# Mamba in-projection: four taps on 128 rows, two chunks in the array's halves, z, B and C padded to full products

## The chip, the cores and the metric

The kernel runs on one core of a Trainium2 chip. The metric is device time in microseconds (us), the median of several runs. Profiles are of one execution each. PE is the matrix engine, PEld its weight load, DVE the vector engine, ACT the scalar engine, POOL GpSimd, SP the engine that issues nearly all of the DMAs. All data is float32, but for the scores' operands, which are float32r.

## The reference

The input x has 4 images of 128 channels and 64 x 64 points. Layer 0 is a group norm, then layer norms, a depthwise 3 x 3 convolution with GELU and a 1 x 1 product, and a Mamba block on four chunks of 32 channels; layer 1 is attention with 4 heads on 4096 tokens and a mixture of 8 experts, of which each token takes 2. The change concerns the Mamba block's beginning. In the reference's words, cut:

```python
xz = u @ in_proj_w.T                      # 32 channels -> 2 * 64
xin, z = jnp.split(xz, 2, axis=-1)
xin = causal depthwise convolution of xin with conv1d_w (4 taps)
xin = jax.nn.silu(xin + conv1d_b)
x_dbl = xin @ x_proj_w.T                  # -> dt (2), B (16), C (16)
delta = softplus(dt @ dt_proj_w.T + dt_proj_b)
h = exp(delta * A) * h + delta * B * xin  # along the 4096 points, for 64 channels x 16 states
y = sum over states of h * C, + D_skip * xin
out = y * silu(z) @ out_proj_w.T
```

The in-projection and the 4 taps can be one product: a weight for each tap, with the input shifted by 0 to 3 points.

## The kernel before

**Blocks, halves, units, slots.** An image is cut into 8 blocks of 512 points (32 blocks in all). The four chunks are taken two at a time: half p = 0, 1 of the 128 channels; a half's two chunks give 2 x 64 inner channels, which fill 128 partitions. In the kernel before, the inner channels of the two chunks alternate over the partitions (`d = slice(c, P, 2)` in `_laid_out`, line 1466). A unit is a block, a half and two of the 16 states: 512 units. The main loop (lines 1363 to 1416) goes through slots, two for each unit, 1024 in all, and further slots for what is left over. In a slot the main loop writes, in this order: DMAs that have been put off (`flush`), a fetch of rows (`fetch`, line 1374), decays on ACT, `driven` on DVE in even slots (h = B row times du), the attention's score products and their exponentials on ACT, the scan on DVE (even), `read` on DVE (odd: hc = C row times h), the first stage of lane Y, transposes of hc summed into y on PE (`turned_on`), the second stage of lane Y, then the weighted sums of the attention (`weighted`, line 982), and a stage of lane X. Every instruction is chained to the one before it on its engine (`queued`, line 387), so this order is the order on each engine, SP's queue among them.

**Lanes.** Work that isn't scan or attention is written as generators whose `yield`s mark stages. Lane Y makes two stages a slot and lane X two; a task starts when it is at the head of its lane and what it names is done. For each block lane Y has `first_norm` (10 stages), `conv` (26) and `inputs` for the two halves (6 each). Lines 1312 to 1330 put them in order: in(k, 1), which waits for the end of the scan of block k-1's half 1, then the first norm of block k+2 (`upper`), the convolution of block k+1, then in(k+1, 0). At an image's first block `upper` stands last, with 14 stages for the group norm. `until` (line 1285) runs the lanes on at once when a fetch needs a half that isn't done.

**In-projection.** `conv` ends with the normalised block xn on 128 channels and sends four copies into `pairs` (lines 647 to 654): for each half p, 64 rows as they are and 64 rows one point later. `send` puts a DMA on SP at the next `flush`. `inputs` (lines 659 to 708) then makes, for half p, the sum of two products with K = 128 (`inxc`, two taps each) into PSUM bank Y, z with K = 64 (`inz`) into bank X, silu of both on ACT, B and C with 64 columns (`wbc`), and dt with 128 columns (`wdt`). B and C go by ACT into `bc`, by a DMA to `bcd` in DRAM, shape (2 chunks, 8, 2, 1024).

**Rows.** For each unit, `fetched` (line 715) reads the two B rows, and in the next slot the two C rows, back from `bcd` to 128 partitions: each partition gets the 1024 values of its chunk. Four buffers (`rows`) serve, and a fetch is issued three slots ahead of its use. There are 1024 such fetches of 512 KB.

```python
in_=in_of[b, i, p][4][:, n // 2, k, :][None].to_broadcast([DI, 2, 2 * BLK]),
```

**Other transfers with a repeated source.** `finished` reads `inv` (line 1042) as 4 heads, each repeated for 32 partitions; `keys` and `share` repeat too.

```python
out=inv, in_=inverse[b, q][u][:, None, :].to_broadcast([NH, DH, BLK])
```

**Attention.** Score products `sc` are 128*128 (weights' rows and columns). The weighted sums `av` are 128*64: two products side by side, to PSUM partitions 0 to 63 and 64 to 127. 

Of the kernel before, what the change touches and what calls it, by code (L numbers as in the profile page):

```python
# [9 lines left out]
F32 = mybir.dt.float32  # L10
# [7 lines left out]
P = 128  # L18
C = 128
EPS = 1e-5  # L20
BLK = 512
NT = BLK // P
IMG = 64
DI = 64
NST = 16
# [11 lines left out]
def conv_mamba_attn_moe_kernel(ctx: ExitStack, tc: tile.TileContext, t: dict):  # L37
# [37 lines left out]

    late = nc.scalar
    gmat, fc1w = (load(k, eng=late) for k in ("gmat", "fc1w"))
    inx, xdt, dtT, alog = (load(k, pool=scratch, eng=late) for k in ("inx", "xdt", "dtT", "alog"))
    cw = load("cw", [P, 4, P], t["cw"].partition_broadcast(P), pool=scratch, eng=late)
    lnw, lnb, fc1b, lcw, lcb = (load(k, eng=late) for k in ("lnw", "lnb", "fc1b", "lcw", "lcb"))  # L80
    fc2T, fc2b, cb, dtb, dsk = (load(k, eng=late) for k in ("fc2T", "fc2b", "cb", "dtb", "dsk"))
    inz, wbc, wout, projT = (load(k, eng=late) for k in ("inz", "wbc", "wout", "projT"))
# [10 lines left out]
        nc.vector.tensor_scalar_mul(taps[:, k, :], ident, fc1w[:, k : k + 1])  # L93


    inxc = const.tile([P, 2, P], F32, name="inxc")
    for j in range(4):
        r = slice(DI * (j % 2), DI * (j % 2) + DI)
        nc.vector.tensor_mul(inxc[r, j // 2, :], inx[r, :], cw[r, j, :])

    amat = const.tile([P, NST], F32, name="amat")
    nc.scalar.activation(amat, alog, AF.Exp)
# [398 lines left out]


    held = set()
    group_of, y0_of, xn_of, pairs_of, in_of, gated, kqv = {}, {}, {}, {}, {}, {}, {}
    IMAGE = "p (r w) -> p r w"
    group_of[0] = gm0, gr0

# [75 lines left out]
    def conv(b, i):  # L583
        cm = tmp("Y", "cm")
        h = work("Y") if b == 0 else cm
        half = b == i == 0

        def tap(k):
            y0 = y0_rows(b, i, k // 3, k % 3)
            w = fc1w[:, k : k + 1]  # L590

            hr = (cm if half and k > 4 else h).rearrange(IMAGE, w=IMG)
            if b == 0 and not (half and k > 4):
                mm(hr, taps[:, k, :], y0, k == 0, k == (4 if half else 8))
            elif k == 0 or half and k == 5:
                vector.tensor_scalar(hr, y0, w, fc1b, ALU.mult, ALU.add)
            else:
                vector.scalar_tensor_tensor(hr, y0, w, hr, ALU.mult, ALU.add)

        for k in range(0, 5 if half else 9, 2):  # L600
            if b:
                yield
            tap(k)
            if k < (4 if half else 8):
                tap(k + 1)
            if half and k < 4:
                tap(k + 5)
                tap(k + 6)
            if b == 0:
                yield  # L610
                if half and k == 4:
                    vector.tensor_add(cm, h, cm)
                elif k == 8:
                    scalar.activation(cm, h, AF.Identity, bias=fc1b)
            yield
        ps = transposed("Y", by_tile(cm))
        yield
        xt = yield from normalised("Y", by_tile(ps))
        ps = transposed("Y", xt)
        yield  # L620
        g = tmp("Y", "g")
        scalar.activation(g, ps, AF.Gelu, bias=lcb, scale=lcw)
        yield
        ps = work("Y")
        mm(ps, fc2T, g)
        yield
        cm = tmp("Y", "cm")
        vector.scalar_tensor_tensor(
            cm.rearrange(IMAGE, w=IMG), ps.rearrange(IMAGE, w=IMG), fc2b, y0_rows(b, i),
            ALU.add, ALU.add,  # L630
        )
        yield
        ps = transposed("Y", by_tile(cm))
        yield
        xt = yield from normalised("Y", by_tile(ps))
        ps = transposed("Y", xt)
        yield

        xn = mix.tile([P, 3 + BLK], F32, name="xn", bufs=3)
        scalar.activation(xn[:, 3:], ps, AF.Identity, bias=lnb, scale=lnw)  # L640
        if i == 0:
            gpsimd.memset(xn[:, 0:3], 0.0)
        else:
            gpsimd.tensor_copy(xn[:, 0:3], xn_of[b, i - 1][:, BLK : BLK + 3])
        xn_of[b, i] = xn

        pairs = mix.tile([P, 2, 2 + BLK], F32, name="pairs")
        for p in range(2):
            for late in range(2):
                send(  # L650
                    pairs[DI * late : DI * late + DI, p, :],
                    xn[DI * p : DI * p + DI, late : late + 2 + BLK],
                )
        pairs_of[b, i] = pairs
        yield
        yield
        yield

    def inputs(b, i, p):

        xn, pairs = xn_of[b, i], pairs_of[b, i]
        r = slice(DI * p, DI * p + DI)
        while held:
            yield
            yield
        held.add("in")
        ps = work("Y")
        summed(ps, [(inxc[:, j, :], pairs[:, p, 2 * j : 2 * j + BLK]) for j in range(2)])
        pz = work("X")
        mm(pz, inz[r, :], xn[r, 3 : 3 + BLK])  # L670
        yield
        xin = mix.tile([P, BLK], F32, name="xin", bufs=2)
        scalar.activation(xin, ps, AF.Silu, bias=cb)
        zs = mix.tile([P, BLK], F32, name="zs", bufs=4)
        scalar.activation(zs, pz, AF.Silu)
        yield

        pb = work("X")
        mm(pb[0:DI, :], wbc, xin)
        ps = work("Y")  # L680
        mm(ps, wdt, xin)
        yield
        held.clear()
        bc = tmp("Y", "bc")[0:DI, :]
        scalar.copy(bc, pb[0:DI, :])
        bcd = dram.tile([2, NST // 2, 2, 2 * BLK], F32, name="bcd", bufs=4)
        send(bcd.rearrange("c n k (m q) -> (c n k m) q", m=2), bc)

        e = tmp("Y", "e")
        scalar.activation(e, ps, AF.Abs, bias=dtb)  # L690
        scalar.activation(e, e, AF.Exp, scale=-1.0)
        ln = tmp("Y", "ln")
        scalar.activation(ln, e, AF.Ln, bias=1.0)
        delta = mix.tile([P, BLK], F32, name="delta", bufs=2)
        scalar.activation(delta, ps, AF.Relu, bias=dtb)
        yield
        yield

        du = mix.tile([P, BLK], F32, name="du", bufs=2)
        lost = du  # L700
        vector.tensor_scalar(lost, e, 1.0, -1.0, ALU.add, ALU.add)
        vector.tensor_sub(lost, e, lost)
        vector.tensor_add(ln, ln, lost)
        vector.tensor_add(delta, delta, ln)
        vector.tensor_mul(du, delta, xin)
        in_of[b, i, p] = xin, zs, delta, du, bcd
        done.add(("in", b, i, p))
        yield
# [6 lines left out]
    def fetched(unit, k):  # L715

        b, i, p, n = unit
        w = mix.tile([P, 2, BLK], F32, name="rows", bufs=4)
        sync.dma_start(
            out=w.rearrange("p m q -> p (m q)"),  # L720
            in_=in_of[b, i, p][4][:, n // 2, k, :][None].to_broadcast([DI, 2, 2 * BLK]),
        )
        return w

# [585 lines left out]

    X.append((("y0", *blocks[1]), first_norm(*blocks[1], "X"), [("y0", *blocks[0])]))
    for k in range(-2, len(blocks)):
        if 0 <= k:
            b, i = blocks[k]
            Y.append((("in", b, i, 1), inputs(b, i, 1), [("scan", *blocks[k - 1], 1)] if k else []))
        if k + 2 < len(blocks):
            b, i = blocks[k + 2]
            if k + 2 == 0 or i > 0:
                upper(k + 2)
        if 0 <= k + 1 < len(blocks):  # L1320
            b, i = blocks[k + 1]
            below = [("y0", b, i + 1)] if i < NB - 1 else []
            Y.append((("xn", b, i), conv(b, i), before(k + 1, 3) + below))
            Y.append((
                ("in", b, i, 0), inputs(b, i, 0),
                before(k + 1, 2) + ([("scan", *blocks[k], 0)] if k >= 0 else []),
            ))

        if 0 < k + 2 < len(blocks) and blocks[k + 2][1] == 0:
            upper(k + 2)  # L1330
# [113 lines left out]
def _laid_out(i):  # L1444
# [10 lines left out]


    def twice(a):
        return np.repeat(a, 2, axis=0)

    z = np.zeros((P, P), np.float32)  # L1460
    inx, inz = z.copy(), z.copy()
    wout = np.zeros((P, 2, P), np.float32)
    wbc = np.zeros((P, 2, NST // 2, 2, 2), np.float32)
    xdt, dtT = np.zeros((4, P), np.float32), np.zeros((4, P), np.float32)
    for c in range(2):
        d = slice(c, P, 2)
        for p in range(2):
            s = slice(64 * p + 32 * c, 64 * p + 32 * c + 32)
            inx[s, d] = c0["in_proj_w"][:DI].T
            inz[s, d] = c0["in_proj_w"][DI:].T  # L1470
            wout[d, p, s] = c0["out_proj_w"].T

        wbc[d, c] = c0["x_proj_w"][2:].reshape(2, NST // 2, 2, DI).transpose(3, 1, 0, 2)
        xdt[2 * c : 2 * c + 2, d] = c0["x_proj_w"][:2]
        dtT[2 * c : 2 * c + 2, d] = c0["dt_proj_w"].T
# [5 lines left out]
    for h in range(NH):  # L1481
# [12 lines left out]
        "lcw": col(c0["lc_ln_w"]), "lcb": col(c0["lc_ln_b"]),  # L1494
        "fc1w": c0["lc_fc1_w"].reshape(C, 9), "fc1b": col(c0["lc_fc1_b"]),
        "fc2T": c0["lc_fc2_w"].T, "fc2b": col(c0["lc_fc2_b"]),
        "inx": inx, "inz": inz,
        "cw": twice(c0["conv1d_w"]).T,
        "cb": col(twice(c0["conv1d_b"])),
        "xdt": xdt, "dtT": dtT, "dtb": col(twice(c0["dt_proj_b"])),  # L1500
        "wbc": wbc.reshape(P, -1), "alog": twice(c0["A_log"]),
# [28 lines left out]
```

## Time and profile before

| what | value |
|---|---|
| median of 3 runs | 5217.45 us (5217.27 to 5228.61) |
| profiled execution | 5213.97 us, its span 5211.8 us |
| PE, DVE, ACT busy | 91%, 74%, 72% |
| mean granted clock of PE | 0.957 |
| DMA: bytes, mean rate | 1131.60 MB, 217 GB/s |
| rows<-bcd | 1024 transfers of 512.0 KB |
| ps_Y<-pairs,inxc | 256 matmul records, busy 131.4 us |
| ps_X<-xn,w_inz | 128 records, 64*128, 74.6 us |
| ps_X<-xin,w_wbc | 128 records, 128*64, 73.0 us |

An f32 product of 512 columns shows as two matmul records. In the lists of instructions "out<-in" are the program's tile names, and "[idle before <-releaser]" is the idle time ahead of an instruction and what ended it. `SPq` rows are DMAs that SP issues.

### The profile page before, as it was taken

The page shows a single profiled execution, that of the slowest core. Times are in us where ns is not written, and L with a number is a line of the kernel's source. Part 1 is how long each engine was busy: PE and PEld are TensorE (multiplying, and loading weights), DVE is VectorE, ACT ScalarE, POOL GpSimd, SP SyncE. Part 2 cuts the span into 40 slices and gives each one's busy share as a digit, 9 for nine tenths or more (in the row PEclk, how much of TensorE's full clock was granted, in tenths as well). Part 3 has the DMA queues.
Part 4 walks back from the last instruction along what each step waited for, and adds up shares of the span by engine and source line. Part 5 has one row for each costly group of instructions (what it writes and reads, how often), then busy time and mean ns, then how long its engine had stood idle before and what let it go on. Part 6 is the DMA issues. An engine that isn't in the chain of part 4 may idle for free.

```text
span 5211.8 us, 62608 instructions
## 1 busy us (share of the span) xinstructions
PE 4743.5 (91%) x20684; PEld 2298.3 (44%) x20684; DVE 3834.8 (74%) x5780; ACT 3749.6 (72%) x5700; POOL 423.0 (8%) x483
## 2 busy tenths in 40 slices
PE   4567899999999999899999999999999999999997
PEld 2333444444444444444444444444444444443443
DVE  6888767777788878888788887887788877751332
ACT  4456777788787787678888787778777787756543
POOL 1111111100000000001000000000000001000000
PEclk7678999999999999899999999999999999999998
DMA  4556567676766667767766667767766666754542
GB/s 126 180 186 207 210 208 244 227 236 242 234 225 228 230 223 239 244 231 246 258 228 226 233 224 231 259 229 253 264 233 228 219 229 219 265 179 156 185 130 72
DMA packets 451692, 1131.60 MB, mean 217 GB/s; under 512 B 51985, under 2 KB 135330, under 8 KB 451362
## 3 DMA queue, kind: packets, MB, share of 16 engines
q1 hardware_dynamic: 447296, 1125.96, 64.4%
q8 instruction: 166, 2.72, 0.2%
q10 hardware_dynamic: 4066, 1.57, 0.2%
q14 instruction: 164, 1.34, 0.1%
HBM read 967.12 MB, written 143.39 MB: 213 GB/s over the span
## 4 chain that ended last, share of the span: by engine, by line
PE 56%; DVE 17%; ACT 13%; DMA 6%; issue 5%; POOL 2%; SPq 1%; DVEq 0%; ACTq 0%; POOLq 0%
PE av L406 23%; PE sc L406 13%; PE ps_X L406 9%; DVE h L406 6%; PE ps_Y L406 5%; PE y L406 5%; ACT pT L406 4%; ACT L406 3%; DMA ks<-kd 2%; DVE hc L406 2%; ACT xt L406 1%; ACT e L406 1%; DMA rows<-bcd 1%; POOL rsX L406 1%; DVE stX L406 1%
## 5 line engine op out<-in xcount | busy, mean ns | idle before, releaser
L406 ACT ACTIVATE pT<-sc 128x1024 f32<-128x1024 f32 x2048 | 1985.0, 1023 | 941.0 <-PE sc L406 939.6
L406 PE MATMUL av<-pT,v 128*64 128x512 f32 x8192 | 2002.9, 610 | 11.4 <-DVE avs L406 11.4
L406 PE MATMUL sc<-qs,ks 128*128 128x512 f32 x4096 | 1294.3, 436 | 67.5 <-DMA ks<-kd 35.8
L406 DVE TENSOR_TENSOR_SCAN h<-da,state,h 128x1025 f32<-128x1025 f32 x512 | 1204.1, 2352 | 96.1 <-ACT h L406 62.5
L406 PEld LDWEIGHTS sc<-qs,ks 128*128 128x128 f32 x4096 | 701.9, 190 | 795.9 <-ACT pT L406 258.1
L406 PEld LDWEIGHTS av<-pT,v 128*64 128x64 f32 x8192 | 500.2, 137 | 846.4 <-issue 816.9
L406 ACT ACTIVATE da<-delta,amat 128x512 f32<-128x512 f32 x1024 | 743.1, 730 | 1.9
L406 PE MATMUL y<-ident,hc 128*128 128x128 f32 x4096 | 628.8, 285 | 64.5 <-DVE hc L406 64.5
L406 DVE TENSOR_TENSOR hc<-rows,h 128x1024 f32<-128x1024 f32 x512 | 624.2, 1219 | 15.8 <-PE y L406 5.9
L406 DVE TENSOR_TENSOR h<-rows,du 128x1024 f32<-128x1024 f32 x512 | 623.4, 1218 | 14.2 <-DMA rows<-bcd 14.1
L406 PEld LDWEIGHTS y<-ident,hc 128*128 128x128 f32 x4096 | 522.8, 147 | 236.9 <-issue 84.6
L406 ACT ACT_TABLE_LOAD x319 | 409.3, 1283 | 19.5 <-DVE zs L406 14.3
L406 POOL TENSOR_TENSOR rsX<-rsX,mhalf 128x4 f32<-128x4 f32 x92 | 203.7, 2214 | 2533.5 <-DVE rsX L406 2448.8
L406 POOL TENSOR_TENSOR rsY<-rsY,mhalf 128x4 f32<-128x4 f32 x100 | 130.6, 1306 | 2070.4 <-DVE shiftY L406 1558.8
L406 DVE TENSOR_TENSOR avs<-av,prev 128x512 f32<-128x512 f32 x96 | 66.1, 689 | 254.2 <-PE av L406 242.8
L406 PE MATMUL ps_X<-share,w_ew 128*128 128x512 f32 x432 | 217.0, 625 | 9.0 <-DVE share L406 8.8
L406 ACT ACTIVATE xt<-ps_Y,shiftY,rsY 128x128 f32<-128x128 f32 x380 | 143.9, 469 | 84.9 <-POOL shiftY L406 77.2
L406 DVE TENSOR_TENSOR share<-share,xf 128x1024 f32<-128x1024 f32 x128 | 155.9, 1218 | 20.5 <-DMA share<-sharesX 14.8
L406 ACT COPY state<-h 128x2 f32<-128x2 f32 x448 | 88.8, 198 | 92.8 <-DVE h L406 92.8
L406 DVE SCALAR_TENSOR_TENSOR cm<-y,w_fc1w,cm 128x512 f32<-128x512 f32 x195 | 144.9, 743 | 8.0 <-ACT y L406 4.5
L406 PE MATMUL ps_Y<-pairs,inxc 128*128 128x512 f32 x256 | 131.4, 638 | 15.0 <-DMA pairs<-xn 9.4
L406 PEld LDWEIGHTS ps_X<-share,w_ew 128*128 128x128 f32 x432 | 74.0, 191 | 149.4 <-issue 97.4
(248 smaller groups left out, 3435.9 us busy)
## 6 DMA issues: line engine op xcount, KB each, us to landing
rows<-bcd SPq DMA_DIRECT2D x1024, 512.0 KB
ks<-kd SPq DMA_DIRECT2D x192, 512.0 KB
qs<-qd SPq DMA_DIRECT2D x161, 512.0 KB
share<-sharesX SPq DMA_DIRECT2D x108, 512.0 KB
v<-vd SPq DMA_DIRECT2D x192, 256.0 KB
ks<-kd SPq DMA_DIRECT2D x128, 256.0 KB
avd<-avs SPq DMA_DIRECT2D x96, 256.0 KB
prev<-avd SPq DMA_DIRECT2D x96, 256.0 KB
```

The lines of the kernel that those rows point to most:

```text
L406: return lambda *args, **kw: queued(op(*args, **kw))
```

## The change

- `inxc` holds one weight [128, 64] in place of two [128, 128]: its rows are 32 channels x 4 taps. `windows` copies, for half p, each chunk's 32 channels with four shifts into 128 rows of `fours`; `conv` sends those of half 0, and `inputs` of half 0 sends those of half 1. The number of sends stays four a block, each of 256 KB.
- `inputs` makes one product of 64 columns for each chunk, to the two halves of PSUM's partitions. A `yield` ahead of it moves it from the first stage of a slot to the second, that is directly ahead of `weighted`. z comes a stage later. A call has 8 stages for 6.
- z's weight has all 128 rows, one matrix for each half, with zeros for the other half. B and C have 128 columns, of which 64 are zeros; only 64 rows of the result are used.
- The inner channels of the two chunks lie one after the other over the partitions (`d = slice(DI * c, DI * c + DI)`). So the source of the rows fetch is written as (2 chunks, 64 repeats, 1024).
- In lane Y, `upper(k + 2)` stands ahead of in(k, 1).

```diff
-    inxc = const.tile([P, 2, P], F32, name="inxc")
-    for j in range(4):
-        r = slice(DI * (j % 2), DI * (j % 2) + DI)
-        nc.vector.tensor_mul(inxc[r, j // 2, :], inx[r, :], cw[r, j, :])
+    inxc = const.tile([P, DI], F32, name="inxc")
+    nc.vector.tensor_mul(inxc, inx, cw)
...
-        pairs = mix.tile([P, 2, 2 + BLK], F32, name="pairs")
-        for p in range(2):
-            for late in range(2):
-                send(
-                    pairs[DI * late : DI * late + DI, p, :],
-                    xn[DI * p : DI * p + DI, late : late + 2 + BLK],
-                )
-        pairs_of[b, i] = pairs
-        yield
-        yield
-        yield
+        windows(b, i, 0)
+        yield
+        yield
+        yield
+
+    def windows(b, i, p):
+        fours = mix.tile([P, 2, BLK], F32, name="fours")
+        for c in range(2):
+            r = slice(DI * p + DI // 2 * c, DI * p + DI // 2 * (c + 1))
+            src = xn_of[b, i][r, :]
+            src = bass.AP(src.tensor, src.offset, (src.ap[0], (1, 4), (1, BLK)))
+            send(fours[:, c, :], src)
+        fours_of[b, i, p] = fours
...
         held.add("in")
+        yield
         ps = work("Y")
-        summed(ps, [(inxc[:, j, :], pairs[:, p, 2 * j : 2 * j + BLK]) for j in range(2)])
-        pz = work("X")
-        mm(pz, inz[r, :], xn[r, 3 : 3 + BLK])
+        for c in range(2):
+            mm(ps[DI * c : DI * c + DI, :], inxc, fours[:, c, :])
         yield
         xin = mix.tile([P, BLK], F32, name="xin", bufs=2)
         scalar.activation(xin, ps, AF.Silu, bias=cb)
+        pz = work("X")
+        mm(pz, inz[:, p, :], xn[:, 3:])
+        yield
         zs = mix.tile([P, BLK], F32, name="zs", bufs=4)
         scalar.activation(zs, pz, AF.Silu)
+        if p == 0:
+            windows(b, i, 1)
         yield
 
         pb = work("X")
-        mm(pb[0:DI, :], wbc, xin)
+        mm(pb, wbc, xin)
...
-            in_=in_of[b, i, p][4][:, n // 2, k, :][None].to_broadcast([DI, 2, 2 * BLK]),
+            in_=in_of[b, i, p][4][:, n // 2, k, :][:, None].to_broadcast([2, DI, 2 * BLK]),
...
-        if 0 <= k:
-            b, i = blocks[k]
-            Y.append((("in", b, i, 1), inputs(b, i, 1), [("scan", *blocks[k - 1], 1)] if k else []))
         if k + 2 < len(blocks):
             b, i = blocks[k + 2]
             if k + 2 == 0 or i > 0:
                 upper(k + 2)
+        if 0 <= k:
+            b, i = blocks[k]
+            Y.append((("in", b, i, 1), inputs(b, i, 1), [("scan", *blocks[k - 1], 1)] if k else []))
...
-        d = slice(c, P, 2)
+        d = slice(DI * c, DI * c + DI)
```

More of the change, by code (lines that the diff above doesn't have):

```diff
@@ L77, in conv_mamba_attn_moe_kernel @@
     gmat, fc1w = (load(k, eng=late) for k in ("gmat", "fc1w"))
-    inx, xdt, dtT, alog = (load(k, pool=scratch, eng=late) for k in ("inx", "xdt", "dtT", "alog"))
-    cw = load("cw", [P, 4, P], t["cw"].partition_broadcast(P), pool=scratch, eng=late)
+    inx, cw, xdt, dtT, alog = (
+        load(k, pool=scratch, eng=late) for k in ("inx", "cw", "xdt", "dtT", "alog")
+    )
     lnw, lnb, fc1b, lcw, lcb = (load(k, eng=late) for k in ("lnw", "lnb", "fc1b", "lcw", "lcb"))
@@ L503, in conv_mamba_attn_moe_kernel @@
     held = set()
-    group_of, y0_of, xn_of, pairs_of, in_of, gated, kqv = {}, {}, {}, {}, {}, {}, {}
+    group_of, y0_of, xn_of, fours_of, in_of, gated, kqv = {}, {}, {}, {}, {}, {}, {}
     IMAGE = "p (r w) -> p r w"
@@ L657, in conv @@
         yield
+    def windows(b, i, p):
[6 more added lines that the diff above has]
+        fours_of[b, i, p] = fours
     def inputs(b, i, p):
-        xn, pairs = xn_of[b, i], pairs_of[b, i]
-        r = slice(DI * p, DI * p + DI)
+        xn, fours = xn_of[b, i], fours_of.pop((b, i, p))
         while held:
@@ L1457, in twice @@
     def twice(a):
-        return np.repeat(a, 2, axis=0)
-    z = np.zeros((P, P), np.float32)
-    inx, inz = z.copy(), z.copy()
+        return np.concatenate([a, a])
+    inz = np.zeros((P, 2, P), np.float32)
     wout = np.zeros((P, 2, P), np.float32)
-    wbc = np.zeros((P, 2, NST // 2, 2, 2), np.float32)
+    wbc = np.zeros((P, 4, NST // 2, 2, 2), np.float32)
     xdt, dtT = np.zeros((4, P), np.float32), np.zeros((4, P), np.float32)
     for c in range(2):
-        d = slice(c, P, 2)
+        d = slice(DI * c, DI * c + DI)
         for p in range(2):
             s = slice(64 * p + 32 * c, 64 * p + 32 * c + 32)
-            inx[s, d] = c0["in_proj_w"][:DI].T
-            inz[s, d] = c0["in_proj_w"][DI:].T
+            inz[s, p, d] = c0["in_proj_w"][DI:].T
             wout[d, p, s] = c0["out_proj_w"].T
@@ L1496, in _laid_out @@
         "fc2T": c0["lc_fc2_w"].T, "fc2b": col(c0["lc_fc2_b"]),
-        "inx": inx, "inz": inz,
-        "cw": twice(c0["conv1d_w"]).T,
+        "inx": np.repeat(c0["in_proj_w"][:DI].T, 4, axis=0), "inz": inz,
+        "cw": np.tile(c0["conv1d_w"].T, (DI // 2, 1)),
         "cb": col(twice(c0["conv1d_b"])),
```

## The prediction

> **What bounds the kernel now.** I read the page's busy times first, then its DMA parts. PE is busy 91% of the span, DVE 74%, ACT 72%; the 16 DMA engines average 64% in the one queue SP feeds.
>
> ```profile
> PE 4743.5 (91%) x20684; PEld 2298.3 (44%) x20684; DVE 3834.8 (74%) x5780; ACT 3749.6 (72%) x5700; POOL 423.0 (8%) x483
> ...
> q1 hardware_dynamic: 447296, 1125.96, 64.4%
> ...
> rows<-bcd SPq DMA_DIRECT2D x1024, 512.0 KB
> ```
>
> The reader is to see two things: PE is nearest to its limit, and half of all bytes (1024 x 512 KB = 537 of 1126 MB) are the rows fetches. Next comes the answer by stages: prologue, scan (slots 0 to 1023, the ones that fetch rows), and the attention left over.
>
> ```profile
> 0.00:73.00 73.00, 31.50 (x110) 16.20 (x110) 27.17 (x112) 16.76 (x30) 11.18 (x40) 0.86 0.28 68
> 73.00:4600.00 4527.00, 4144.49 (x18328) 2040.77 (x18330) 3637.71 (x5203) 3430.39 (x5335) 399.21 (x430) 0.96 0.69 230
> 4600.00:5212.00 612.00, 567.47 (x2248) 241.34 (x2244) 169.92 (x466) 302.44 (x336) 12.60 (x13) 0.96 0.41 136
> ```
>
> Columns: stretch, us, then busy us of PE, PEld, DVE, ACT, POOL, granted clock, DMA share, GB/s. A slot of the scan lasts 4527/1024 = 4.42 us, and PE has 4.05 us of work in it. DMA is 69% busy and spread over 16 engines, so rows is rarely late: the waits of DVE show it last only 7 times, 14.1 us in all. Third, the timeline of PE around one in-projection:
>
> ```profile
> 2422.49 1.19 PE L406 MATMUL sc<-qs,ks 128*128 128x512 f32 x4
> 2423.53 1.88 PE L406 MATMUL ps_Y<-pairs,inxc 128*128 128x512 f32 x4
> 2425.33 1.12 PE L406 MATMUL ps_X<-xn,w_inz 64*128 64x512 f32 x2
> 2426.39 1.94 PE L406 MATMUL av<-pT,v 128*64 128x512 f32 x8
> 2428.25 1.20 PE L406 MATMUL sc<-qs,ks 128*128 128x512 f32 x4
> 2429.38 1.07 PE L406 MATMUL ps_X<-xin,w_wbc 128*64 128x512 f32 x2
> 2430.38 1.13 PE L406 MATMUL ps_Y<-xin,wdt 128*128 128x512 f32 x2
> 2431.35 1.47 PE L406 MATMUL y<-ident,hc 128*128 128x128 f32 x12
> ```
>
> Two records are one f32 product. Start to start, PE never idles here; these slots are PE's. Last, the answer on the tile inv, because its source has the shape that the changed rows fetch gets (below):
>
> ```profile
> L406 SPq DMA_DIRECT2D inv<-inverse x32: 517/557/832, 1311.2 to 5156.6; - x32
> ...
>   DMA inv<-inverse: 61.7, 20
> ```
>
> DVE stood still 61.7 us for these 32 transfers of 256 KB, more than four times what 1024 rows transfers cost it.
>
> **What the Trainium skill says.** "DMA: Bandwidth & Descriptors", section "Why a DMA increments its semaphore by 16 and not by 1": a transfer is split over k engines, k being the largest number up to 16 that divides the sizes of the slowest dimension (other than 1) of both access patterns, and only those k engines post a completion. The trace agrees. Counting the completion events after each issue, the trace has 16 for every rows, ks, aT and share transfer, 9 for sharesX<-prT (8 rows), and 5 for inv<-inverse, total<-avs and den<-total, whose slowest dimension is 4: k engines and one write by the issuer. The same page, section "Rules for kernel authors", warns that an outermost dimension of c < 16 confines the whole DMA to at most c engines. "TensorEngine Tiling (Array Packing)", section "Key Properties": tiles run in parallel, and changing the tiling mode drains the array. The trace agrees: two av products side by side take 1.86/2 = 0.93 us (2426.39 to 2428.25 for two such pairs), hardly more than one full product (1.80/2 = 0.90 us), and w_inz (64*128) takes 1.06.
>
> **The change, part by part.**
>
> *Taps in the array's halves.* Two full products (1.80 us) become one pair in halves, placed by the added yield directly ahead of av, which has the same 128*64 mode: 0.93 us and no further switch. Saves 0.87 us for each of 64 calls.
>
> *z, B, C padded.* w_inz 1.06 to 0.90, saves 0.16. w_wbc stood between full products: sc before it ran 1.13 instead of some 1.04, it took 1.00 and wdt 0.97; full, 1.80 for both: saves 0.26. Together 1.29 us x 64 = 83 us of PE. PE is idle 468 us of the span, so not each of these slots is PE's; at about two thirds it is worth 55 us, if PE stays the bound. From both sides: 0 to 83.
>
> *Windows.* Per block SP issues four transfers as before (two per half), of 256 KB instead of 128.5 KB: 512 packets of 2048 B (median 84 ns) for 256. 256 more x 32 blocks x 84 ns / 16 = 43 us more per DMA engine. Their sources have 32 partitions, so 16 engines. The second half's pair is issued from inside the first call, which ends two slots later; the call for it then waits for the scan anyway. Free at today's 69%. PE waited 9.4 us for pairs in all; the mm now comes half a slot later, so no more than that.
>
> *Two more stages a call, order of the lane.* Lane Y makes two stages a slot, 64 a block, and needs 52 instead of 48. upper(k+2) fills the wait for the scan that head-of-lane in(k,1) had. At the three batch borders in(.,1) ends about the slot where it is fetched; at most a few us each. I take 0; below zero at most some 10 us.
>
> *Set-up.* One multiplication for four, 0.9 us less on DVE; inx and cw 256 KB smaller, inz and wbc 96 KB larger. 0.
>
> *Rows.* The halves of the partitions now hold the two chunks one after the other, so the source of rows<-bcd goes from (64 repeats, 2 chunks, 1024) to (2 chunks, 64 repeats, 1024). This is inv's form, (4 heads, 32 repeats, 512), with 2 in place of 4. So k goes from 16 to 2: each of two engines moves 64 packets of 4096 B instead of 8. A 4096 B packet takes 159 ns (median; 10th percentile 156; mean 195, with 16 engines competing). The packets in flight at once never stay much above 16, so an engine serves one at a time. One fetch: 64 x 159 ns = 10.2 us, against a slot of 4.42 us that needs one fetch. It can't be hidden by more buffers: it is throughput. Four rows buffers keep two or three fetches queued on these two engines, so they hardly starve.
>
> **The sum for the two engines in the scan.** Rows: 1024 x 10.18 = 10,420 us. All else that they carry: 0.69 x 4527 = 3,124 us of packets per engine now, less rows' own 131,072 x 195 ns / 16 = 1,594, is 1,530; at the uncontended 159/195 of that, 1,250. The k = 4 transfers already lie on the low engines (24 packets more than an even share for each of 64 total and some 27 inv): 24 x 91 x 84 ns = 183. The windows: 43. Sum 11,896 us. With prologue 73 and the tail 612, whose slots fetch no rows: 12,581. Idle of the two engines: SP waits in order for a transfer's landing before it can issue the next (bcd before rows 64 times, sharesX, total, inverse 32 times each or less, 160 chains); such a landing now queues behind rows ("DMA: Bandwidth & Descriptors", "Queues, rings and completion order": each engine takes its descriptors in ring order; no view of before shows a queue that long). Nothing at best, one fetch each at worst, 160 x 10.2 = 1,630. I take a quarter, 400, since the scan's calls are mostly done several slots ahead of their fetch. 12,980; less what PE saves in the tail, 0. The profiled execution has 5211.8 us of span and 2.2 around it, 5213.97 in all, 3.5 (0.07%) under the median of 5217.45, far below the uncertainty here. Forecast: **12,980 us**.
>
> Low end: packets at 156 ns (10,224) and no idle: 12,385, say 12,300. High end: all chains drain, 12,581 + 1,630 = 14,210, and some gap between packets: 14,400.
>
> **The rivals.**
>
> *Faster: rows keeps its 16 engines.* If destination and source are split jointly in a way that inv doesn't show, the change is what its words say, and PE's 83 us are worth two thirds: 5,214 - 55 = 5,159 us. The mechanism's place is the split of the 1024 fetches; it decides from k = 8: 32 KB x 2 a fetch, 16 x 159 ns = 2.5 us, plus 1.4 us of other traffic, 3.9 us, fits the 4.42 us slot; at k = 4 5.1 + 1.4 us don't. Against it: inv, total and den, all three. Chance 0.04.
>
> *Starved engines.* k = 2, but the chains drain at each landing and the FIFO order delays ks and v behind three fetches (30 us, where they are asked for three slots ahead), so PE and with it hc are late too: 14,400 to 16,500, say 15,200 us. For it: one queue, in order. Against it: rows waits only for DVE, and DVE's and PE's work of a slot is 4 us of nearly 12. Chance 0.09.
>
> *More than two engines at a time or faster packets:* a split over 4 (5.1 us of rows) gives 73 + 1024 x 5.09 + 1,476 + 612 = 7,370 us. For it only that a form not seen may be split otherwise. Chance 0.03. Within 0.3% is left with 0.01.
>
> The forecast's own case has 0.83; within it the range above. Chances: faster by over 0.3% 0.04, within 0.3% 0.01, slower 0.95 (0.3% is about what a measurement of this kernel can tell from no change).
>
> **What would show it.** Right: 3 completion events for each rows transfer; DMA rows<-bcd as the wait of DVE's h and hc by thousands of us (1024 x some 7 us); PE busy below 40%; the DMA rows at 1 to 2 tenths through the scan, about 88 GB/s on average, and the tail as long as now; ps_Y<-fours pairs starting about 0.93 us before av, w_inz and w_wbc at 0.90. A slot of the scan near 12 us. Wrong: 16 events, or PE still near 91% (first rival); idle stretches of DMA in the scan of more than 10% of it (second). The lane's steps are wrong if PE waits for fours more than 10 us in all before any rows are late.

## The result, and the profile after

| | median us | ratio to before, 95% |
|---|---|---|
| before | 5217.36 (5214.05 to 5228.61, 6 runs) | 1 |
| changed | 12880.01 (12874.39 to 12886.01, 6 runs) | 2.4686 (2.4661 to 2.4711) |
| forecast | 12,980, range 12,300 to 14,400 | |

The change made the kernel 2.47 times as slow. The same parts of the page that were read before, for the changed kernel: busy times, the DMA line of the 40 slices, the queue's share, and the chain that ended last.

```profile
PE 5585.2 (43%) x20684; PEld 2729.1 (21%) x20684; DVE 3890.8 (30%) x5777; ACT 3777.0 (29%) x5700; POOL 396.6 (3%) x483
...
DMA  1111222222222222222222222222222222223243
...
q1 hardware_dynamic: 441152, 1142.62, 25.9%
...
DMA 64%; SPq 20%; PE 9%; DVE 5%; ACT 1%; issue 1%; POOL 0%; DVEq 0%; ACTq 0%; POOLq 0%
```

DVE and ACT have the work that they had (3891 for 3835 us, 3777 for 3750), and PE has the same 20684 records, which take 5585 us for 4744 at a lower clock. No engine got more to do; they wait. The trap is the DMA line: 2 tenths look like an idle resource. A mean over 16 engines of 2 tenths is also what two full engines and fourteen nearly empty ones give, and the chain says DMA for 64% and SP's queue (SPq) for 20%. By stages, with the columns as in the prediction:

```profile
0.00:73.00 73.00, 30.87 (x110) 15.94 (x110) 26.59 (x110) 18.29 (x32) 11.18 (x40) 0.86 0.29 73
73.00:12200.00 12127.00, 4960.92 (x18254) 2459.52 (x18256) 3680.89 (x5193) 3445.25 (x5318) 372.82 (x430) 0.68 0.25 87
12200.00:12881.00 681.00, 593.44 (x2322) 253.66 (x2318) 183.27 (x474) 313.42 (x351) 12.61 (x13) 0.92 0.39 133
```

The whole loss is in the scan; prologue and tail are as they were (the last rows fetch is issued at 12,241.5, so 42 us of the last line still belong to the scan). PE's mean granted clock fell to 0.68 in the scan; how its clock goes with its pauses is taken up at the end of the experiments. The answer on the tile rows, the fetches and then DVE's waits for them, first before, then after:

```profile
L406 SPq DMA_DIRECT2D rows<-bcd x1024: 512/519/1810, 73.1 to 4591.4; - x171
...
  DMA rows<-bcd: 14.1, 7
```

```profile
L405 SPq DMA_DIRECT2D rows<-bcd x1024: 487/3427/17143, 71.6 to 12241.5; - x171
...
  DMA rows<-bcd: 4690.6, 674
```

DVE waits for rows 674 times, 4691 us in all, where it waited 7 times, 14.1 us. The lines of the fetches (min, median and max in ns) hold what I had not looked for: to issue one such transfer takes SP 3.4 us in the median instead of 0.52.

Three counts from the trace's lists of DMA packets and completion events. The packets in flight are those of the queue that SP feeds, over the scan, which I take from 73 us to 12,253 us, 11.5 us after the last fetch is issued:

```
completion events a rows transfer   before 16    after 3 (two engines and the issuer)
packet of 4096 B, median            159 ns       160 ns
packets in flight, after            2: 9241 us   0 or 1: 61 us   3 and more: 2878 us
```

For three quarters of the scan exactly two packets are in flight: two engines work, fourteen have nothing to do.

### The profile page after: what moved, and what is told of

Same layout as the page of the kernel before. It is cut to its first block, busy times and chain, and to the rows that moved or that the text cites. A ratio compares the mean times of both kernels' runs of the same rounds, so it can differ in the third digit from the quotient of the medians.

```text
span 12880.9 us, 62527 instructions
## 1 busy us (share of the span) xinstructions
PE 5585.2 (43%) x20684; PEld 2729.1 (21%) x20684; DVE 3890.8 (30%) x5777; ACT 3777.0 (29%) x5700; POOL 396.6 (3%) x483
## 4 chain that ended last, share of the span: by engine, by line
DMA 64%; SPq 20%; PE 9%; DVE 5%; ACT 1%; issue 1%; POOL 0%; DVEq 0%; ACTq 0%; POOLq 0%
DMA rows<-bcd 37%; SPq L405 20%; DMA ks<-kd 10%; PE av L405 4%; DMA sharesX<-prT 3%; PE sc L405 3%; DMA fours<-xn 2%; DMA inv<-inverse 2%; DMA share<-sharesX 2%; DMA gn<-in_x 2%; DVE h L405 2%; DMA xr<-in_xtok 2%; PE ps_X L405 1%; DMA prev<-avd 1%; PE ps_Y L405 1%
## 5 line engine op out<-in xcount | busy, mean ns | idle before, releaser
L405 PE MATMUL sc<-qs,ks 128*128 128x512 f32 x4096 | 1518.4, 500 | 3785.4 <-DMA ks<-kd 3773.9
L405 PE MATMUL av<-pT,v 128*64 128x512 f32 x8192 | 2316.9, 689 | 16.5 <-DVE avs L405 15.7
L405 PEld LDWEIGHTS sc<-qs,ks 128*128 128x128 f32 x4096 | 847.6, 228 | 4620.3 <-issue 4062.3
L405 PE MATMUL y<-ident,hc 128*128 128x128 f32 x4096 | 781.0, 331 | 943.7 <-DVE hc L405 839.2
L405 PEld LDWEIGHTS y<-ident,hc 128*128 128x128 f32 x4096 | 635.9, 174 | 1222.9 <-DVE hc L405 892.4
L405 PEld LDWEIGHTS av<-pT,v 128*64 128x64 f32 x8192 | 597.3, 157 | 1059.0 <-issue 1026.2
L405 PE MATMUL ps_X<-share,w_ew 128*128 128x512 f32 x432 | 267.9, 752 | 371.7 <-DVE share L405 371.7
L405 PE MATMUL ps_Y<-fours,inxc 128*64 128x512 f32 x256 | 136.0, 978 | 394.2 <-DMA fours<-xn 394.2
L405 ACT COPY h<-state 128x1 f32<-128x1 f32 x512 | 97.8, 191 | 615.6 <-DVE hc L405 615.5
L405 PE MATMUL ps_X<-w_wp,aT 128*128 128x128 f32 x216 | 51.6, 414 | 410.4 <-DVE aT L405 410.4
```

Of the source, the lines that this page charges most:

```text
L405: return lambda *args, **kw: queued(op(*args, **kw))
```

## Experiments: is it the rows fetch's split?

The theory: the split of the rows fetch over two engines is the whole loss, as throughput. Rivals: other edits of the change have a part in it; the order of the one queue and its latencies set the time.

**One line put back.** The source's repeats outside again, in the changed kernel.

```diff
-            in_=in_of[b, i, p][4][:, n // 2, k, :][:, None].to_broadcast([2, DI, 2 * BLK]),
+            in_=in_of[b, i, p][4][:, n // 2, k, :][None].to_broadcast([DI, 2, 2 * BLK]),
```

> The changed kernel with one line put back: the rows fetch's source is again (64 repeats, 2 chunks, 1024). The two chunks then reach the partitions in turn, while the changed layout has them one after the other, so this kernel multiplies partly by the other chunk's B and C; number and size of all instructions are those of the changed kernel. Theory (the loss is the split of the rows fetch over two engines, all else of the change saves PE time): 16 completion events a transfer, 5159 us, between 5110 and 5215. Rival (windows, stages or lane order lose something too): over 5220 us. Rival (the line has nothing to do with it): near 12880 us.

Measured: 5215.12 us, ratio 0.9994 (0.9985 to 1.0003), 16 events a transfer. The line is the loss. That the time is at the very end of the theory's range (5215), with no gain at all, is the subject of the next section.

**The line and its layout alone,** in the kernel before.

```diff
-            in_=in_of[b, i, p][4][:, n // 2, k, :][None].to_broadcast([DI, 2, 2 * BLK]),
+            in_=in_of[b, i, p][4][:, n // 2, k, :][:, None].to_broadcast([2, DI, 2 * BLK]),
...
-        return np.repeat(a, 2, axis=0)
+        return np.concatenate([a, a])
...
-        d = slice(c, P, 2)
+        d = slice(DI * c, DI * c + DI)
```

> The kernel before with only the chunks laid one after the other over the partitions and the rows fetch as (2 chunks, 64 repeats, 1024). Theory (two engines carry all rows): as slow as the whole change, 12800 to 13000 us, with two packets in flight for some 9200 us of the scan. Rival (the other edits take a good part of the loss): below 11000 us. Rival (the line is harmless): near 5217 us.

Measured: 12,922.49 us (one run), two packets in flight for 9378 us up to the last fetch's issue. Taps, padding, windows and stages have no part in the loss.

**Four and eight engines.** Each row of bcd is written two or four times, so that the source's outermost dimension is 4 or 8 (here for two copies):

```diff
-        bcd = dram.tile([2, NST // 2, 2, 2 * BLK], F32, name="bcd", bufs=4)
-        send(bcd.rearrange("c n k (m q) -> (c n k m) q", m=2), bc)
+        bcd = dram.tile([NST, 2, 2, 2, BLK], F32, name="bcd", bufs=4)
+        for c in range(2):
+            for m in range(2):
+                send(
+                    bcd[:, c, :, m, :],
+                    bc[32 * c + m : 32 * c + 32 : 2, None, :].to_broadcast([NST, 2, BLK]),
+                )
...
+            in_=in_of[b, i, p][4][n + k].rearrange("c r m q -> (c r) (m q)")[:, None]
+            .to_broadcast([4, 32, 2 * BLK]),
...
```

> The changed kernel, with each B and C row written twice to DRAM, so that the source of a rows fetch is (2 chunks x 2 copies, 32 repeats, 1024): slowest dimension 4. Theory (throughput of k engines, 64/k x 2 packets of 159 ns an engine and fetch): 5 completion events, 1024 x 5.1 us of rows and some 1750 us of other packets on the low engines, with prologue and tail 7650 us, between 7350 and 7900. Rival (latency or the order of the queue, not the engines' throughput, sets the time): well over 8500 us, since all waits in order stay. Rival (split doesn't matter): 12880 us.

> The changed kernel with each B and C row written four times: slowest dimension 8. Theory (throughput of k engines): 9 completion events; rows 1024 x 2.55 us and some 1900 us of other packets on the low eight engines are 4500 us, just what the scan of the 16-engine kernels takes, so 5350 to 5700 us. Rival (order and latency set the time, as their waits are the same for each k): over 6000 us.

Measured, one run each: 7925.87 us with 5 events, and 6125.23 us with 9. The events are as expected; both times lie past my ranges, four engines by 26 us and eight by 425 us, where the rival's "over 6000 us" is what came. So the times alone don't decide; what the traces have in flight does. Up to the last fetch, exactly k packets are in flight for 9241 us (k = 2), 4257 us (k = 4) and 2007 us (k = 8): each doubling takes away more than half, as throughput must. Fewer than k are in flight for only 61, 104 and 380 us of the scan, so the k engines stay full and latency sets little of the time. And more than k are in flight, with other traffic beside the rows, for 2878, 2864 and 3042 us; this hardly changes, and with eight engines it is over half of the scan. My sums took 1750 and 1900 us for all other packets and 159 ns for a packet of 4096 B, which took 191 and 227 ns in the mean. With eight engines the fetch isn't hidden; DVE's h still waited 235.8 us for it.

**Sixteen engines by copies, and two fetches.** Eight copies in the way shown (outermost 16), or no copies and a fetch for each chunk:

```diff
-        sync.dma_start(
-            out=w.rearrange("p m q -> p (m q)"),
-            in_=in_of[b, i, p][4][:, n // 2, k, :][:, None].to_broadcast([2, DI, 2 * BLK]),
-        )
+        for c in range(2):
+            sync.dma_start(
+                out=w[DI * c : DI * c + DI].rearrange("p m q -> p (m q)"),
+                in_=in_of[b, i, p][4][c, n // 2, k, :][None].to_broadcast([DI, 2 * BLK]),
+            )
```

> The changed kernel, with each B and C row written eight times to DRAM, so that the source of a rows fetch is (2 chunks x 8 copies, 8 repeats, 1024). Theory (engine count): 16 completion events and the PE part of the change comes through, 5170 us, between 5110 and 5230; the copies add 57 MB of writes, some 150 us of the 16 engines' time in a scan that has room. Rival (reading one row many times in a run is slow by itself): over 5500 us.

> The changed kernel with each rows fetch issued as two transfers of 64 partitions, one for each chunk, each from a single row repeated 64 times. Theory (engine count): both have 16 completion events; as fast as with the repeats outside, 5215 us, plus what 1024 more issues of some 0.52 us on SP's queue cost: between 5205 and 5260. Rival (two half-height transfers on the same engines are slower in themselves, as the eightfold copies were): over 5300 us.

Measured: 5342.41 us, ratio 1.0254 (1.0236 to 1.0271), and 5340.64 us, ratio 1.0238 (1.0222 to 1.0254). Both have 16 events and are rid of the loss, but for some 125 us, which put both over my ranges (up to 5230 and 5260). In both, a packet of 4096 B took longer, 241 and 243 ns on average for 194 with the repeats outside. I took that for the price of engines that read one row over and over, and tried it in the changed kernel:

```diff
-            in_=in_of[b, i, p][4][:, n // 2, k, :][:, None].to_broadcast([2, DI, 2 * BLK]),
+            in_=in_of[b, i, p][4][0, n // 2, k, :][None].to_broadcast([P, 2 * BLK]),
```

> The changed kernel with every rows fetch reading one row (the first chunk's) 128 times, in one transfer over 16 engines; the second chunk's channels get the first's B and C. Theory (packets slow down when engines read one row over and over: 241 ns for 4096 B in the copies, 243 in the two fetches, 194 with the two rows in turn): 5340 us, packets of 240 ns. Rival (the half-height transfers and the copies each have their own cost): 5215 us, packets of 195 ns.

Measured: 5216.79 us, ratio 0.9999 (0.9991 to 1.0008), packets 195 ns. That theory fell. What the copies and the half-height transfers pay 125 us for stays open; that both share one cause isn't shown either.

## Experiments: where did PE's gain go?

With the line put back, PE's shorter products are there, and the time is that of before. The timeline of PE in that kernel:

```profile
2414.49 1.08 PE L405 MATMUL ps_Y<-fours,inxc 128*64 128x512 f32 x4
2415.40 1.89 PE L405 MATMUL av<-pT,v 128*64 128x512 f32 x8
2417.22 1.20 PE L405 MATMUL sc<-qs,ks 128*128 128x512 f32 x4
2418.25 1.02 PE L405 MATMUL ps_X<-xn,w_inz 128*128 128x512 f32 x2
2419.11 1.47 PE L405 MATMUL y<-ident,hc 128*128 128x128 f32 x12
...
2424.58 1.02 PE L405 MATMUL ps_X<-xin,w_wbc 128*128 128x512 f32 x2
2425.44 1.02 PE L405 MATMUL ps_Y<-xin,wdt 128*128 128x512 f32 x2
2426.30 0.60 PE L405 MATMUL y<-ident,hc 128*128 128x128 f32 x4
```

From start to start the pair in halves, z, B and C, and dt take 0.91, 0.86, 0.86 and 0.86 us, 3.49 for the 4.83 of before (1.80, 1.06, 1.00, 0.97). By this one call the estimate is 1.34 x 64 = 86 us. But PE's busy time fell by 55 us only, at a mean clock of 0.950 for 0.957 (by estimate 0.007 x 5216 = 37 us), and its idle time grew from 468 to 528 us. Four kernels take the edits apart.

**Lane order as before,** in the kernel with the line put back:

```diff
+        if 0 <= k:
+            b, i = blocks[k]
+            Y.append((("in", b, i, 1), inputs(b, i, 1), [("scan", *blocks[k - 1], 1)] if k else []))
         if k + 2 < len(blocks):
             b, i = blocks[k + 2]
             if k + 2 == 0 or i > 0:
                 upper(k + 2)
-        if 0 <= k:
-            b, i = blocks[k]
-            Y.append((("in", b, i, 1), inputs(b, i, 1), [("scan", *blocks[k - 1], 1)] if k else []))
```

> The changed kernel with the repeats outside (5215 us), and lane Y's order as in the kernel before: in(k, 1) ahead of the next first norm. Theory (PE's 95 us went into later waits because slots are also bound by ACT and DVE, whatever the order of the lane): 5205 to 5225. Rival (the new order moved norms to slots where PE waits for them, 122 us for xt instead of 69): 5150 to 5190.

**Six stages as before,** in the same kernel:

```diff
         held.add("in")
-        yield
         ps = work("Y")
...
+        pz = work("X")
+        mm(pz, inz[:, p, :], xn[:, 3:])
         yield
         xin = mix.tile([P, BLK], F32, name="xin", bufs=2)
         scalar.activation(xin, ps, AF.Silu, bias=cb)
-        pz = work("X")
-        mm(pz, inz[:, p, :], xn[:, 3:])
-        yield
```

> The changed kernel with the repeats outside (5215 us), and the six stages of the kernel before: taps and z at once in the first stage of a slot, not next to the weighted sums. The pair in halves then stands between full products, some 0.1 us a call more on PE. Theory (PE's gain is lost in any case): 5205 to 5230. Rival (the two added stages cost what PE gained): 5150 to 5190.

**Both edits.**

> The changed kernel with the repeats outside (5215 us), and both the six stages and the lane order of the kernel before: of the change there remain the windows, the taps in halves, the padding and the layout, and every stage falls where it fell before. Theory (the moved stages, by either edit, eat PE's 95 us, since slots have other limits): 5125 to 5175 us, below the 5185 us of the padding alone. Rival (windows and halves gain nothing wherever they stand): 5185 us or more.

**The padding alone,** in the kernel before:

```diff
-        mm(pz, inz[r, :], xn[r, 3 : 3 + BLK])
+        mm(pz, inz[:, p, :], xn[:, 3:])
...
-        mm(pb[0:DI, :], wbc, xin)
+        mm(pb, wbc, xin)
...
```

The rest of this edit makes the two weights larger and fills them with zeros.

> The kernel before with only z's weight on 128 rows and B and C's on 128 columns, padded with zeros; order, layout and fetches as before. PE has 0.16 + 0.26 us less for each of 64 calls, 27 us. Theory (little of PE's gain reaches the end of a slot): 5205 to 5218. Rival (the padding's gain is real and the moved stages eat it in the whole change): 5185 to 5200.

| kernel | us | ratio, 95% | POOL busy us | rsY power, median ns | PE idle us | PE busy at half clock, us |
|---|---|---|---|---|---|---|
| before | 5217 | 1 | 423.0 | 1007 | 468 | 300 |
| padding alone | 5184.80 | 0.9936 (0.9922 to 0.9950) | 423.4 | 1008 | 473 | 284 |
| line put back, stages and order of before | 5185.15 | 0.9935 (0.9922 to 0.9949) | 423.0 | 1007 | 487 | 271 |
| line put back | 5215.12 | 0.9994 (0.9985 to 1.0003) | 455.3 | 1981 | 528 | 353 |
| line put back, order of before | 5217.65 | 0.9997 (0.9988 to 1.0005) | 494.7 | 1918 | 517 | 385 |
| line put back, six stages | 5228.05 | 1.0015 (1.0009 to 1.0022) | 515.3 | 1919 | 517 | 338 |

Two things follow. The padding brings 33 us, all of what PE saves by it (its busy time falls by 34 us): where nothing is moved, PE's time counts nearly one for one, and my theory for that run (little reaches the end of a slot) was wrong. And windows with taps in halves bring nothing beyond it where they stand between full products, as the rival of that run had it; there the pair takes 1.00 and 1.53 us in two calls and not 0.91. With the added stages, or with the new order, or with both, the kernel loses the padding's gain as well, 30 to 43 us. That these two edits take the gain is shown; by what way is less clear.

The table shows a first candidate, POOL. Lane Y's norms raise the variance to the power -0.5 there. The answer on the tile rsY, first before, then with the line put back (min/median/max ns):

```profile
L406 POOL TENSOR_TENSOR rsY<-rsY,mhalf x100: 1006/1007/1992, 22.7 to 5168.4; 128x4 f32<-128x4 f32 x100
```

```profile
L405 POOL TENSOR_TENSOR rsY<-rsY,mhalf x100: 1007/1981/1992, 21.0 to 5168.5; 128x4 f32<-128x4 f32 x100
```

The Trainium skill, "SBUF — State Buffer", section "Who interferes with whom", says that a DVE instruction with two SBUF inputs contends with a GpSimd instruction that reads SBUF. The traces agree: a power took 1.9 to 2.0 us where a DVE product of two SBUF tiles (hc, h, share) was running when it began, 1.0 us beside none of these (43 of 44 powers before), and 1.0 to 1.5 us where the power began first. Before, 27 of the 100 powers met such a product running, with the line put back 65: the moved stages put the norms there. PE's wait for xt, the norm's next step, went from 68.8 to 122.0 us. To price it, the padding alone got a second, unused power ahead of the real one in lane Y:

```diff
+        if lane == "Y":
+            junk = small.tile([P, NT], F32, name="junk")
+            gpsimd.tensor_tensor(junk, rs, mhalf, ALU.pow)
         gpsimd.tensor_tensor(rs, rs, mhalf, ALU.pow)
...
```

> The padding alone (5185 us), with a second power of -0.5 on POOL, its result unused, ahead of the real one in lane Y's norms, 95 times: each adds 1.0 us to the way from DVE to ACT's xt, or 2.0 us where it falls beside a DVE product of two SBUF tiles. Theory (where the moved stages put 72 instead of 39 of the 100 powers beside such a product, these 33 x 1 us cost the 30 to 40 us that are missing; time on POOL in the norms counts nearly one for one): 5250 to 5340 us. Rival (the longer powers are a by-product, the norms have slack): below 5200 us.

Measured: 5254.40 us, ratio 1.0070 (1.0054 to 1.0086), 70 us over the padding alone for 133 us more on POOL. The waits of PE, first of the padding alone, then with the second power:

```profile
PE ps_Y L406 <- ACT xt L406: 69.6, 21, 7.7
PE y L406 <- DVE hc L406: 64.6, 21, 9.2
```

```profile
PE ps_Y L406 <- ACT xt L406: 139.6, 50, 10.1
PE y L406 <- DVE hc L406: 65.0, 21, 9.2
```

PE's wait for xt grew by 70 us. In the two profiled executions, which are 74 us apart, PE's idle time grew by 62 us (473 to 535) and its busy time by 12. So in this kernel a us on POOL costs about half a us; my theory's "nearly one for one" was too much, though the time is just inside its range. By that price the 32, 72 and 92 us more of POOL in the last three rows of the table would be 17, 38 and 48 us, against 30, 33 and 43 us lost.

The waits do not bear this out for the last two. The second power showed up as PE's wait for xt. This wait is 122.0 us with the line put back, where it is 70.2 with stages and order of before, but only 80.3 with the order of before and 97.7 with six stages. (For the first of the three it would do: 52 us more, where PE's idle time grew by 41.) What grew most in the other two is another wait each. First with stages and order of before, then with the order of before alone, then with six stages alone:

```profile
PE sc L405 <- ACT pT L405: 46.4, 140, 2.2
PE ps_X L405 <- DVE bothX L405: 39.6, 25, 4.0
```

```profile
PE sc L405 <- ACT pT L405: 87.2, 90, 3.5
```

```profile
PE ps_X L405 <- DVE bothX L405: 77.5, 24, 4.1
```

Of the waits over 2.5 us between 600 and 4600 us, 20 are for pT with the order of before and 19 for bothX with six stages; with both edits undone they are 0 and 4. In the first case ACT has dt's softplus (e, ln, delta) ahead of the exponentials, as at 1506 to 1512 us; in the second DVE works through the router's small instructions, as at 1714 to 1718 us. So POOL is one place of several where the moved stages make PE pause, and its price is shown for the second power alone.

A pause also costs more than its length. In all traces of this case PE's granted clock is either full or half, and the half comes in stretches of 3.4 us or multiples of it (but for the last one, which the trace's end cuts). In the kernels of the table and the one with the second power, 120 of the 151 pauses of PE of 2.5 us or more, between 600 and 4600 us, meet a stretch at half clock that begins during them or within 10 us after; a window of such a length taken anywhere meets one in 10% of cases. So the table's last two columns go together: against the row with stages and order of before, the last three have 30 to 41 us more of idle time and 67 to 114 us more of products at half clock, whose half, 33 to 57 us, is by estimate what the slower clock adds. Both are of the size of what is lost. No run holds one of the two still, so how the loss divides between them is open.

## Why the prediction was right, step by step

- **Rows, k from 16 to 2, 10.2 us a fetch:** right. 3 events a transfer, 160 ns a packet, two in flight, and the line alone gives all of the loss, both ways.
- **Sum for the two engines, 11,896 us:** the scan took 12,180 us, 12,119 without the idle time, so the sum was 223 us short. How that divides between rows and all else is not shown, as a packet's record names its queue and not its engine. Part of it is in the rows' term: I had taken the median of 159 ns, but where the rows run alone (stretches of 8 us and more with at most three packets in flight) the mean is 161.5 ns, which makes 10,585 us where I had 10,420, and would leave 1,534 us for all else instead of 1,476. That the transfers of four engines lie on these same two isn't shown either. The "10th percentile 156" of my low end was misread: 156 ns is the shortest packet of this size, the 10th percentile is 159.
- **Idle 400 us:** 61 us. The chains of transfers that wait for each other did not drain the two engines. This error of 339 us and the 223 us of the sum have opposite signs; that forecast and median are only 100 us apart is in part luck and no test of either.
- **Prologue 73 and tail 612:** 73 and 628 (from 12,253 to the end; the last fetch lands at 12,268, which leaves 613).
- **Signs:** DVE waited thousands of us for rows, but 4,691 and not the 7,200 of "1024 x some 7 us", and 879 us for PE's av beside them. PE busy "below 40%" did not come: it was 43%, as its products took longer at the lower clock. With the line put back PE waited 6.3 us for the windows, under the 10 I had named.
- **PE's 83 us a call's products, two thirds of it real:** the size was right (86 by one call), the share wrong: none with the rows mended, 0.9994 (0.9985 to 1.0003). The step that failed is "Two more stages a call, order of the lane", with its "I take 0". Its cover, twelve spare stages in the lane, was there; what I had not priced was where in a slot the moved work falls on POOL, ACT and DVE, and that PE then pauses and runs on at half clock. The stages and the order cost 30 us against the kernel without them, with 41 us more of PE's idle time.
- **Rivals.** Faster with 16 engines: excluded for the change, and as a hypothesis too hopeful (5215, not 5159). Its point of decision was wrong: eight engines are not enough, 6125 us. Starved engines: excluded by 61 us of idle. PE does wait 3774 us for ks, which stands behind rows in the queue, but as the two engines are full meanwhile, this sets no time of its own. A split over four engines: 3 events exclude it.

## What to carry to other kernels

A DMA's access pattern is a choice of engines: write it with an outermost dimension that is a multiple of 16 on both sides (16, 64 and 128 had 16 completion events here; 2, 4 and 8 had 3, 5 and 9), and check the number of these events, since the average DMA share hides a transfer that sits on two engines. When a layout change forces a small outer dimension into a transfer, price that transfer before anything else. And a stage moved to where its engine has room can still cost time through what runs ahead of it or beside it on another engine: compare the waits and the durations of the same instructions before and after, and on PE the time at half clock.

## What the runs showed that I had not expected

- SP stood still in issuing: median 3.4 us for a rows transfer on two engines, up to 17.1, against 0.52; 11.5 ms of SP's time for all its transfers, against 1.6. Transfers over 16 engines behind them took longer to issue as well (qs 4.8 us against 0.54, ks 1.5 against 0.54): a full pair of engines holds up the queue that feeds all sixteen.
- Two ways to give the chunk-by-chunk layout its 16 engines back cost 2.4 and 2.5%, with packets of 241 and 243 ns instead of 194, and reading a single row for all partitions costs nothing.
- A POOL power of 128 x 4 elements takes 1.0 us, or 2.0 when a DVE product from SBUF is running as it begins; of 133 us more of POOL's time, 70 reached the end.
- Most pauses of PE of 2.5 us or more (120 of 151) go with a stretch at half clock, so that moved work can cost PE twice.
- The padding alone, which computes nothing new, beats the kernel before: 5184.80 us, ratio 0.9936 (0.9922 to 0.9950).
